# Layer 0's mixture of experts computed by lists of chosen tokens instead of for every token and expert

## The chip, the cores and the metric

The kernel runs on one core of a Trainium2 chip. A core has five engines that run side by side, each with its own queue of instructions: PE (TensorE, matmuls), DVE (VectorE), ACT (ScalarE), POOL (GpSimd) and SP (SyncE, which here mostly issues DMA). The metric is the device time of one execution in microseconds (us), the median over several runs. Times inside an execution come from a hardware profile of one further execution, counted from the start of its span.

## The reference

The whole is a decoder of four layers over 1024 tokens (8 blocks of 128, in two halves of 512) of 128 features. Each layer is an attention, a cross attention and a feed-forward part, and after each comes a sum with the input and a layer norm. The part that changes is layer 0's feed-forward part, a mixture of 8 experts of which each token uses two:

```python
def _L0_ffn_ref(x, router_w, w13, w2):
    E, H, I, K = (8, 128, 256, 2)
    logits = jnp.einsum('bsh,eh->bse', x, router_w)
    probs = jax.nn.softmax(logits, axis=-1)
    weights, indices = jax.lax.top_k(probs, K)
    weights = weights / (weights.sum(axis=-1, keepdims=True) + 1e-06)
    h13 = jnp.einsum('bsh,ehi->bsei', x, w13)
    gate, up = jnp.split(h13, 2, axis=-1)
    h = jax.nn.silu(gate) * up
    y = jnp.einsum('bsei,eih->bseh', h, w2)
    y_sel = jnp.take_along_axis(y, indices[..., None], axis=2)
    return (y_sel * weights[..., None]).sum(axis=2)
```

Layer 2 has a mixture of the same kind (8 experts, two per token, inner width 448). After layer 0's mixture come layer 1's attention over rotated vectors (`a1` in the code) and its cross attention with 16 heads (`x1`, computed by `attention16`).

## The kernel before, in words

Only PE's order is written out by hand (`manual_schedule(engines={PE})` around `first_layers`): PE runs in the order of the program. The queues of the other engines are put in order by the compiler, which takes the order of the program as priority and its own estimate of when an operand is ready. An instruction that waits holds up everything behind it on its engine.

**Layer 0's cross attention**, `ContextAttention`, runs in 35 units, u = 0 to 34, four for each block of 128 tokens; its last three only fold the last block's heads together and norm half 1 (L391 and L345 to L351 on DVE).

**Layer 0's mixture**, `FirstExperts` (L864 to L912), is dense: all 8 experts for all tokens, as 16 items, an expert and a half of 512 tokens each. `up` makes four matmuls with 512 columns (L889 to L891), a silu on ACT (L893) and a product on DVE (L894). `down` makes 8 matmuls of 128 columns (L904), and DVE adds the four results times the router's weight, zero where the expert isn't chosen, to an accumulator (L907). The weights come in four DMAs of 768 KB long before they are used. `top2` makes the router's weights. Items 0 to 3 run in the units u = 31 to 34; then a loop over k = 4 to 16 does one item's `up` and the item before's `down` in each step, and has other work between: x0's second turn after k = 5, the second half's routing, layer 1's 4-bit weights (`wq`) and constants after k = 6, the norm of half 0 after k = 8, and layer 1's rotated attention for half 0 (`a1.project`, `values`, `scores`, `turned`, `outputs`, `f.turn`) after k = 9 to 15. After the loop come `moe.norm(1)` and `x1.queries(0)`, then `attention16`, whose callback `between` holds half 1 of `a1`.

**Layer 2's mixture**, `ListedExperts` (L915 to L1126), takes only chosen pairs of a token and an expert, for each half on its own:

- `rows` writes the half's 512 input rows to DRAM. `route` finds each token's two experts. `places` counts by matmuls how many tokens chose each expert, and gives each pair a slot in a list in which every expert's part begins at a multiple of 128: at most N8 = 15 items of 128 rows. Its one-hot tiles `s16` and `r16` go into `lists`, whose 8 matmuls turn them into the ids of the rows of each item, and which then issues 15 gathers on POOL (L1030), an indirect DMA of 128 rows each into `e_xg` (8 buffers).
- For an item, `loaded` reads the expert's number into a register of SP and loads that expert's weights (L1043, four items ahead), `turned` transposes the gathered rows (L1060) and copies them by ACT (L1065), `up` and `down` compute the expert (silu L1075, product L1077), and the result goes to DRAM (L1088).
- `sums` gathers each token's two results back, 8 gathers on POOL (L1114), and 8 operations on DVE add them by weight to the input (L1122).

`run` (L1090) does the 30 items with other steps between them, among them `sums(0)` after item 17.

Of the kernel before, what the change touches and what calls it, by code (L numbers as in the profile page):

```python
# [21 lines left out]
B = 8  # L22
# [120 lines left out]
C2 = M2 // 4  # L143
W2COLS = 2 * M2 + 4 * D
# [10 lines left out]
W0COLS = 2 * I0 + 2 * D  # L155
# [3 lines left out]
def tile_decoder(  # L159
# [293 lines left out]

    def top2(xt, rw, eps, bs=range(B)):

        n = len(bs)

        def few(tag, shape, bufs=2):
            return small.tile(shape, F32, tag=f"{tag}{n}", name=tag, bufs=bufs)

        lg = ps_out.tile([P, n, 8], F32, tag="out", name="ps_lg")
        for k, b in enumerate(bs):
            mm(lg[:, k, :], tok(xt, b), rw)
        pr = softmax8(lg)
        shape = [P, n, 8, 8]
        other = pr.unsqueeze(2).to_broadcast(shape)
        own = pr.unsqueeze(3).to_broadcast(shape)
        gt = work.tile([P, B, 8, 8], F32, tag="g_gt", name="g_gt", bufs=1)[:, :n]
        nc.vector.tensor_tensor(gt, other, own, ALU.is_gt)
        eq = work.tile([P, B, 8, 8], F32, tag="g_eq", name="g_eq", bufs=1)[:, :n]  # L470
        nc.vector.tensor_tensor(eq, other, own, ALU.is_equal)
        eqf = eq.rearrange("p b e j -> p b (e j)")
        nc.vector.tensor_tensor(eqf, eqf, repeat(cst("tri"), n), ALU.mult)
        nc.vector.tensor_tensor(gt, gt, eq, ALU.add)
        rank = few("g_rank", [P, n, 8])
        nc.vector.tensor_reduce(rank, gt, AX.X, ALU.add)
        sel = few("g_sel", [P, n, 8])
        nc.vector.scalar_tensor_tensor(sel, rank, 2.0, pr, ALU.is_lt, ALU.mult)
        sm = few("g_sm", [P, n])
        nc.vector.tensor_reduce(sm, sel, AX.X, ALU.add)  # L480
        if eps:
            nc.vector.tensor_scalar_add(sm, sm, eps)
        rs = few("g_rs", [P, n])
        nc.vector.reciprocal(rs, sm)
        w = few("g_w", [P, n, 8], 8 // n)
        nc.vector.tensor_tensor(w, sel, spread(rs, 8), ALU.mult)
        return w
# [376 lines left out]
    class FirstExperts:  # L864


        def __init__(self, pool, x, xT):
            self.pool, self.xT, self.hT = pool, xT, {}
            self.f = Finish(x, of=third)
            self.acc = tile_of(pool, "e_acc", [P, B, D], bufs=1)  # L870
            nc.gpsimd.memset(self.acc, 0.0)
            self.w, self.loaded = {}, {}

        def load(self):
            for e in range(0, E0, 2):
                t = stream.tile([P, 2, W0COLS], F32, tag="w", name="w_moe0")
                nc.sync.dma_start(out=t, in_=w_moe0[:, e : e + 2, :])
                self.loaded[e // 2] = t

        def route(self, i):  # L880
            self.w[i] = top2(self.xT, msc("rw0"), 1e-6, range(4 * i, 4 * i + 4))

        def up(self, k):
            i, e = divmod(k, E0)
            t = self.loaded[e // 2][:, e % 2, :]
            h = tile_of(self.pool, "e_h", [P, 2, 512])
            for c in range(2):
                pg = ps_mm.tile([P, 512], F32, tag="mm", name="ps_g")
                mm(pg, t[:, c * P : (c + 1) * P], half(self.xT, i))  # L889
                pu = ps_sc.tile([P, 512], F32, tag="sc", name="ps_u")  # L890
                mm(pu, t[:, I0 + c * P : I0 + (c + 1) * P], half(self.xT, i))  # L891
                g = tile_of(self.pool, "e_g", [P, 512])
                nc.scalar.activation(g, pg, AF.Silu)  # L893
                nc.vector.tensor_tensor(h[:, c, :], g, pu, ALU.mult)  # L894
            self.hT[k] = h

        def down(self, k):
            i, e = divmod(k, E0)
            h = self.hT.pop(k)
            down = self.loaded[e // 2][:, e % 2, 2 * I0 :].rearrange("p (c d) -> p c d", d=D)  # L900
            po = ps_out.tile([P, 4, D], F32, tag="out", name="ps_o")
            for j in range(4):
                for c in range(2):
                    mm(po[:, j, :], h[:, c, j * T : (j + 1) * T], down[:, c, :], c == 0, c == 1)  # L904
            for j in range(4):
                a = self.acc[:, 4 * i + j, :]
                nc.vector.scalar_tensor_tensor(  # L907
                    a, po[:, j, :], self.w[i][:, j, e : e + 1], a, ALU.mult, ALU.add
                )

        def norm(self, i):
            self.f.norm(i, self.acc[:, 4 * i : 4 * i + 4, :])  # L912


    class ListedExperts:  # L915

# [42 lines left out]
        def places(self, i):  # L968
# [36 lines left out]
            for j in range(1, 4):  # L1005
                for k in range(2):
                    nc.gpsimd.tensor_scalar(self.r16[:, 4 * k + j, 1, :], item[:, 4 * k + j, :], float(j), None, ALU.mult)
            for k in range(2):
                nc.gpsimd.memset(self.r16[:, 4 * k, 1, :], 0.0)
# [1372 lines left out]
```

## Time and profile before

| | us |
|---|---|
| median of 11 runs | 875.99 (871.75 to 881.05) |
| the profiled execution's own time | 876.89 |
| its span | 875.1 |
| mean TensorE clock granted | 0.923 of full speed |
| busy over the span: PE | 724.7 (83%) |
| DVE | 545.2 (62%) |
| ACT | 418.5 (48%) |
| POOL | 177.6 (20%) |
| x0's last norm, from the folding's end to the normed rows | 165.8 to 173.4 |
| attention16's first scores | 251.49 |
| layer 2's last down ends | 690.0 |
| layer 2's mixture, normed rows of half 1 | 708.32 |

A line of the trace's timeline gives start and duration in us, the engine, the line of the source (helpers have one line for all their uses: L297 is every matmul, L329 a transpose of four), the output and the inputs by their names in the program, shapes, and how many such instructions are taken together. In square brackets stands how long the engine stood idle before it, and what ended that. PE is matmuls, PEld its loads of weights. A clock of 0.98 is the mean that the throttle granted in a stretch, as a share of full speed.

### The profile page before, as it was taken

The page shows a single profiled execution, that of the slowest core. Times are in us where ns is not written, and L with a number is a line of the kernel's source. Part 1 is how long each engine was busy: PE and PEld are TensorE (multiplying, and loading weights), DVE is VectorE, ACT ScalarE, POOL GpSimd, SP SyncE. Part 2 cuts the span into 40 slices and gives each one's busy share as a digit, 9 for nine tenths or more (in the row PEclk, how much of TensorE's full clock was granted, in tenths as well). Part 3 has the DMA queues.
Part 4 walks back from the last instruction along what each step waited for, and adds up shares of the span by engine and source line. Part 5 has one row for each costly group of instructions (what it writes and reads, how often), then busy time and mean ns, then how long its engine had stood idle before and what let it go on. Part 6 is the DMA issues. An engine that isn't in the chain of part 4 may idle for free. (4 is left out here: it accounts for less than half of the span.)

```text
span 875.1 us, 14577 instructions
## 1 busy us (share of the span) xinstructions
PE 724.7 (83%) x4790; PEld 497.1 (57%) x4790; DVE 545.2 (62%) x1561; ACT 418.5 (48%) x963; POOL 177.6 (20%) x373
## 2 busy tenths in 40 slices
PE   8789999999988687349888879769998869888883
PEld 4678776665655444125345445458997626655552
DVE  4767786674476665888777766653324166656663
ACT  3233455333566663454186555625334323566662
POOL 1400000010011300001120203044442220066660
PEclk9779999999999799769999999979998979999998
DMA  9310000000000000000000000056897274011111
GB/s 356 124 37 1 1 1 1 1 1 0 1 1 1 1 1 1 1 0 1 0 1 1 1 1 1 13 190 174 265 300 219 76 304 188 1 34 35 36 34 41
DMA packets 22771, 53.57 MB, mean 61 GB/s; under 512 B 3904, under 2 KB 14144, under 8 KB 21280
## 3 DMA queue, kind: packets, MB, share of 16 engines
q1 hardware_dynamic: 20640, 47.55, 16.2%
q0 software_dynamic: 1472, 3.02, 1.4%
q10 hardware_dynamic: 576, 2.00, 0.6%
q8 instruction: 39, 0.64, 0.3%
q14 instruction: 44, 0.36, 0.1%
HBM read 46.39 MB, written 3.01 MB: 56 GB/s over the span
## 5 line engine op out<-in xcount | busy, mean ns | idle before, releaser
L534 DVE TENSOR_REDUCE at_mx<-ps_s 128x8 f32<-128x1024 f32 x48 | 56.9, 1218 | 42.2 <-PE ps_s L297 42.2
L537 ACT ACTIVATE at_s<-ps_s,at_mx 128x128 f32<-128x128 f32 x192 | 53.7, 389 | 38.1 <-DVE at_mx L534 38.1
L297 PE MATMUL ps_o<-w_moe,e_h 128*128 128x128 f32 (+1 forms) x496 | 64.6, 279 | 8.6 <-DVE e_h L1077 5.9
L297 PEld LDWEIGHTS ps_o<-w_moe,e_h 128*128 128x128 f32 (+1 forms) x496 | 61.0, 194 | 17.0 <-issue 8.6
L546 ACT ACTIVATE at_pT<-ps_T 128x512 f32<-128x512 f32 x96 | 53.8, 601 | 34.3 <-PE ps_T L329 34.0
L329 PE MATMUL ps_T<-const_sb,at_s 128*128 128x128 f32 x384 | 61.9, 300 | 6.9 <-ACT at_s L537 5.1
L297 PE MATMUL ps_idle<-begin_bf 128*128 128x512 bf16 x226 | 63.9, 423 | 3.2 <-DVE l_s L658 2.2
L2119 POOL COPY l_wg<-w 128x64 f32 x192 | 48.6, 299 | 82.9 <-ACT l_wd L2115 54.5
L329 PEld LDWEIGHTS ps_T<-const_sb,at_s 128*128 128x128 f32 x384 | 47.5, 149 | 28.6 <-issue 10.7
L297 PEld LDWEIGHTS <-begin_bf 128*128 128x128 bf16 x273 | 28.0, 111 | 62.3 <-issue 41.9
L1077 DVE TENSOR_TENSOR e_h<-e_g,ps_u 112x512 f32<-112x512 f32 x30 | 20.6, 688 | 57.8 <-PE ps_u L297 45.4
L297 PEld LDWEIGHTS ps_acc<-l_wd,l_h 128*128 128x128 f32 x256 | 31.0, 191 | 38.5 <-ACT l_h L2141 38.5
L297 PE MATMUL ps_acc<-l_wd,l_h 128*128 128x128 f32 x256 | 37.1, 288 | 13.3 <-ACT l_h L2141 13.3
L805 ACT ACTIVATE x_p<-ps_s,x_mx 128x256 f32<-128x256 f32 x64 | 30.0, 475 | 33.7 <-DVE x_mx L801 26.1
L517 POOL TENSOR_TENSOR kx<-xa_k,const_sb 128x512 f32<-128x512 f32 x16 | 16.8, 1054 | 130.1 <-PE ps_s L297 74.0
L2115 ACT COPY l_wd<-w 64x128 f32 x96 | 28.5, 297 | 26.1 <-PE ps_acc L297 19.1
L297 PE MATMUL ps_s<-kvT,x_q 128*128 128x256 f32 x128 | 35.6, 404 | 4.0 <-ACT x_p L805 4.0
L297 PE MATMUL ps_av<-at_pT,vaug 128*32 128x128 f32 x768 | 31.1, 284 | 9.0 <-ACT at_pT L546 8.5
L335 ACT ACTIVATE sd<-ln_mv,eps 128x4 f32<-128x4 f32 x28 | 8.3, 298 | 62.7 <-DVE ln_mv L346 55.3
L894 DVE TENSOR_TENSOR e_h<-e_g,ps_u 128x512 f32<-128x512 f32 x32 | 21.8, 685 | 24.0 <-PE ps_u L297 20.8
L893 ACT ACTIVATE e_g<-ps_g 128x512 f32<-128x512 f32 x32 | 19.0, 597 | 34.2 <-PE ps_g L297 28.1
L1030 POOL DMA_INDIRECT e_xg<-l_rows,e_ids x30 | 29.1, 971 | 29.3 <-PE ps_T L1060 16.3
(481 smaller groups left out, 1720.4 us busy)
## 6 DMA issues: line engine op xcount, KB each, us to landing
w_moe<-in_w_moe_dram SPq DMA_DIRECT2D x30, 704.0 KB
w<-in_w_moe_dram SPq DMA_DIRECT2D x10, 1024.0 KB
w_moe<-in_w_moe_dram SPq DMA_DIRECT2D x4, 768.0 KB
l_wd<-w SPq DMA_DIRECT2D x96, 32.0 KB
l_out<-e_y SPq DMA_DIRECT2D x30, 64.0 KB
sq_sb<-in_squares_dram SPq DMA_DIRECT2D x1, 1152.0 KB
row_sb<-in_rows_dram ACTq DMA_DIRECT2D x1, 784.0 KB
const_sb<-in_consts_dram ACTq DMA_DIRECT2D x1, 630.5 KB
```

What stands on the lines that cost most here:

```text
L297: nc.tensor.matmul(dst, lhsT, rhs, start=start, stop=stop)
L329: nc.tensor.transpose(ps[:, i, :], src[:, i, :], ident)
L534: nc.vector.tensor_reduce(nmx[k], flat, AX.X, ALU.max, negate=True)
L537: nc.scalar.activation(sh[u][1][:, i // 4, i % 4, :], flat[:, i, :], AF.Identity, bias=nmx[1][:, i : i + 1])
L546: to_T(sh[u][g // 2][:, g % 2], lambda t: nc.scalar.activation(p, t, AF.Exp))
L805: nc.scalar.activation(pr[:, j, :], ps[:, j, :], AF.Exp, bias=mx[:, j : j + 1], accum_out=sm[:, j : j + 1])
L893: nc.scalar.activation(g, pg, AF.Silu)
L894: nc.vector.tensor_tensor(h[:, c, :], g, pu, ALU.mult)
L1030: nc.gpsimd.indirect_dma_start(out=xg, out_offset=None, in_=self.rows_d[i], in_offset=bass.IndirectOffsetOnAxis(ap=self.ids[i][:, o : o + ...
L1077: nc.vector.tensor_tensor(self.h[k], g, pu[:C2], ALU.mult)
L2115: nc.scalar.copy(dst, src)
L2119: nc.gpsimd.tensor_copy(dst, src)
```

## The change

`FirstExperts` and `top2` go. `ListedExperts` gets the inner width and the size of a chunk as arguments and serves both layers. For layer 0 an item is 128 gathered rows: a load of 384 KB, a transpose, 4 up matmuls and 2 down matmuls of 128 columns; 30 items for the two halves. The gathered rows of the second half get buffers of their own, 12 of them, in both layers (before, both halves shared 8). The `r16` products move from POOL to DVE, `s16` comes after them. `run` becomes `step(k)`, and `first_layers` places the steps:

```diff
-                    if u == 21:
-                        moe = FirstExperts(pool_of("l0f", 2, "right"), x0.f.x, x0.f.xT)
-                        moe.load()
-                    if u == 22:
-                        moe.route(0)
...
+                    if u == 18:
+                        moe.rows(0, xin[:, 0:4, :])
+                    elif u == 22:
+                        moe.route(0, x0.f.xT)
+                    elif u == 25:
+                        moe.places(0)
+                    elif u == 28:
+                        moe.lists(0)
                     if u >= 4 * B - 1:
-                        moe.up(u - 4 * B + 1)
-                        if u >= 4 * B:
-                            moe.down(u - 4 * B)
+                        moe.step(u - 4 * B + 1)
+                moe.rows(1, xin[:, 4:8, :])
+                moe.weights_of(0)
                 x1 = None
-                for k in range(4, 2 * E0 + 1):
-                    if k < 2 * E0:
-                        moe.up(k)
-                    moe.down(k - 1)
+                for k in range(4, 2 * N8 + 1):
+                    moe.step(k)
                     if k == 5:
                         x0.f.turn(1)
                     elif k == 6:
-                        moe.route(1)
+                        moe.route(1, x0.f.xT)
...
-                    elif k == 8:
-                        moe.norm(0)
-                    elif k == 9:
-                        moe.f.turn(0)
                     elif k == 10:
-                        a1.project(0)
-                        a1.values(0)
-                    elif k == 11:
-                        a1.scores(0)
+                        moe.places(1)
...
+                        x1.keys(0)
                     elif k == 12:
-                        a1.turned(0)
-                        x1.keys(0)
-                    elif k == 13:
-                        a1.outputs(0)
-                    elif k == 15:
-                        a1.f.turn(0)
-                        x1.biased(0)
-                moe.norm(1)
+                        moe.second = pool_of("l0g", 1, "right")
+                        moe.lists(1)
+                        x1.keys(1)
+                    elif k == N8 + 2:
+                        f.norm(0, moe.sums(0, xin[:, 0:4, :]))
+                        moe.weights_of(1)
+                    elif k == N8 + 11:
+                        f.turn(0)
+                    elif k == N8 + 12:
+                        a1.project(0)
+                        a1.values(0)
+                    elif k == N8 + 13:
+                        a1.scores(0)
+                f.norm(1, moe.sums(1, xin[:, 4:8, :]))
+                idle(6)
+                a1.turned(0)
+                a1.outputs(0)
+                idle(20)
+                a1.f.turn(0)
+                x1.biased(0)
                 x1.queries(0)
...
-                        (0, 1): (lambda: x1.keys(1),),
-                        (0, 2): (lambda: moe.f.turn(1), lambda: a1.project(1)),
-                        (1, 0): (lambda: a1.values(1),),
+                        (1, 0): (lambda: f.turn(1), lambda: a1.project(1), lambda: a1.values(1)),
```

`idle(n)` puts n matmuls on PE whose result nobody reads. Inside `ListedExperts`, for both layers:

```diff
-            self.s16 = work.tile([P, 8, P], BF16, tag="g_gt", name="e_s16", bufs=1)
-            nc.vector.tensor_tensor(self.s16, spread(s, P), repeat(tidx, 8), ALU.is_equal)
...
-            nc.gpsimd.tensor_scalar(self.r16[:, :, 0, :], item, cst("index"), None, ALU.mult)
-            for j in range(1, 4):
-                for k in range(2):
-                    nc.gpsimd.tensor_scalar(self.r16[:, 4 * k + j, 1, :], item[:, 4 * k + j, :], float(j), None, ALU.mult)
...
+            nc.vector.tensor_scalar(self.r16[:, :, 0, :], item, cst("index"), None, ALU.mult)
+            nc.vector.tensor_tensor(
+                self.r16[:, :, 1, :].rearrange("p (k j) o -> p k j o", j=4),
...
+            nc.vector.tensor_tensor(self.s16, spread(s, P), repeat(tidx, 8), ALU.is_equal)
...
-                self.xg[N8 * i + o] = xg = self.few("xg", [P, D], bufs=8)
+                self.xg[N8 * i + o] = xg = (self.second if i else self.pool).tile(
+                    [P, D], F32, tag=f"e_xg{i}", name="e_xg", bufs=12 if i else 8
+                )
...
-            t = stream.tile([P, 1, W2COLS], F32, tag="w", name="w_moe8")
+            t = stream.tile([P, 1, 2 * self.inter + self.n * D], F32, tag="w", name="w_moe8")
```

In the new code the loads of an item's weights are issued four items ahead, as in layer 2, from the four big loads' place at the kernel's start nothing is left. The host packs layer 0's weights by expert as it did layer 2's.

## The prediction

> **What bounds the kernel now.** I first read the windows view over the two mixtures: layer 0's dense one (from the end of the units without mixture, 146.50, to attention16's first scores, 251.49) and layer 2's, which already runs by lists.
>
> ```profile
> core 0: us, PE busy (x) PEld busy (x) DVE busy (x) ACT busy (x) POOL busy (x), PEclk, DMA share, GB/s
> 146.50:251.50 105.00, 101.64 (x477) 64.76 (x476) 63.02 (x189) 47.04 (x78) 5.51 (x11) 0.98 0.00 1
> 592.00:690.00 98.00, 88.69 (x773) 86.71 (x772) 33.30 (x86) 40.10 (x96) 34.94 (x41) 0.96 0.74 226
> ```
>
> The dense stage is PE's alone: 101.64 of 105.00 us busy at clock 0.98, no DMA. Everything else hides behind it. The listed stage uses DMA at 0.74 and POOL for a third. I therefore price the new stage with layer 2's rows. The PE timeline gives one dense item (176.12 back to the same point of the previous one, 170.91: 5.21 us), the second block one listed item of layer 2 (2.75 us).
>
> ```profile
> 174.34 1.95 PE L297 MATMUL ps_o<-w_moe,e_h 128*128 128x128 f32 x16
> 176.12 1.02 PE L297 MATMUL ps_g<-x_T,w_moe 128*128 128x512 f32 x2
> 176.99 1.02 PE L297 MATMUL ps_u<-x_T,w_moe 128*128 128x512 f32 x2
> ```
>
> ```profile
> 669.52 0.28 PE L1060 MATMUL ps_T<-const_sb,e_xg 128*128 128x128 f32 x1
> 669.63 1.03 PE L297 MATMUL ps_g<-e_xT,w_moe 128*112 128x128 f32 x8
> 670.51 1.04 PE L297 MATMUL ps_u<-e_xT,w_moe 128*112 128x128 f32 x8
> 671.38 1.06 PE L297 MATMUL ps_o<-w_moe,e_h 112*128 112x128 f32 x8
> 672.27 0.27 PE L1060 MATMUL ps_T<-const_sb,e_xg 128*128 128x128 f32 x1
> ```
>
> A matmul counts as two entries (x8 for four), so the listed item is a transpose (0.11) and 12 matmuls of 0.22.
>
> **What PE loses.** 16 dense items × 5.21 = 83.4 us go. 30 listed items with 256 inner columns come: 0.11 + (4 up + 2 down) × 0.22 = 1.43, × 30 = 42.9. PE sheds 40.5 us. Would the rest keep up, the kernel would end near 836. So I follow the chain of results that no longer hides.
>
> **A. Units 18 to 30 (to 146.5).** Places and lists of half 0 are new there: PE +0.36 and +0.42 (their matmuls in layer 2), DVE +4.0 net (4.9 for places' row in layer 2 with s16 on top, less the 0.9 of the weights that go and the adds that move). DVE is busy 20.28 of the 24.1 us from 122, so some 4 us are free, but not always where they are wanted. Bounds 0.8 (PE alone) to 6 (all of DVE in the way); I take 2: first item at 148.5.
>
> **B. To the end of x0's folding.** x0's own PE part is 5.4; steps 0 to 2 are 3.96 (three items, their first down later). End 148.5 + 9.4 = 157.9, against 165.8 now.
>
> **C. To the second half's ids.** The chain is a row of links that layer 2 and layer 0 show: norm of half 1, 165.8 to 173.4 now, 7.6 (PE has only steps 3 to 5, 4.3, so it stands 3.4 us ahead of the turn); turn 1.2; step 6, 1.43; route 0.8; then PE's wq transposes 2.5, steps 7 to 10 5.7 and the exp/silu table pair 2 (the item around such a pair in layer 2 took 4.67 instead of 2.75), 10.2 together, which is more than route's DVE chain of 7.0 (187.0 to 194.03 now); places 0.36; its chain to s16 4.9 (613.9 to 618.8); lists 0.42; ids 0.75. Sum 27.7: ids at 185.7 (t0).
>
> **D. To the last down.** POOL's queue now holds 15 row gathers of half 1 (12 free buffers, so the first 12 start at once) and then sums(0)'s 8. A gather costs POOL 0.95 and 0.30 between, 1.25; 23 × 1.25 = 28.75. The whole-engine timeline of layer 2 shows what hangs behind them:
>
> ```profile
> 652.17 0.35 DVE L1122 SCALAR_TENSOR_TENSOR fin_h<-e_y,e_w,l_xx 128x128 f32<-128x128 f32 x1 [2.24 <-DMA e_y<-l_out,e_place]
> ...
> 655.20 0.35 DVE L1122 SCALAR_TENSOR_TENSOR fin_h<-e_y,e_w,l_xx 128x128 f32<-128x128 f32 x1 [2.68 <-DMA e_y<-l_out,e_place]
> 656.42 0.94 POOL L1114 DMA_INDIRECT e_y<-l_out,e_place  x1 [0.30 <-issue]
> ...
> 659.90 0.69 DVE L1077 TENSOR_TENSOR e_h<-e_g,ps_u 112x512 f32<-112x512 f32 x1 [2.48 <-remote]
> ...
> 660.65 0.58 PE L297 MATMUL ps_o<-w_moe,e_h 112*128 112x128 f32 x1 [5.46 <-DVE e_h L1077]
> ```
>
> Adds that wait for gathers stand ahead of e_h in DVE's queue, and PE stood 5.46 us. In the new stage an item is half as long, so the gathers are later against PE. From the last gather's start to the norm's end layer 2 takes 6.1 (702.24 to 708.32): f.norm(0) ends at t0 + 27.5 + 6.1 = t0 + 34. PE has by then only steps 13 to 26 (20 us): it stands 13 us, in pieces of an add each. Then turn 1.2, steps 27 to 30 5.7, project 1.73, values 0.9, scores 0.9, the last item's lag 1.5: t0 + 46 = 231.7. PE's work alone would be 29 (all of it without a wait), the bound from below; 48.5 with more of it at the low clock.
>
> **E. The tail, to attention16.** Now sums(1) gathers after the last down, where before there was no gather at all. DVE in layer 2's tail (last down ended at 690.0):
>
> ```profile
> 696.01 0.35 DVE L1122 SCALAR_TENSOR_TENSOR fin_h<-e_y,e_w,l_xx 128x128 f32<-128x128 f32 x1 [7.27 <-DMA e_y<-l_out,e_place]
> ...
> 702.25 0.35 DVE L1122 SCALAR_TENSOR_TENSOR fin_h<-e_y,e_w,fin_h 128x128 f32<-128x128 f32 x1 [0.39 <-DMA e_y<-l_out,e_place]
> 702.52 0.18 DVE L346 BATCH_NORM_AGGREGATE ln_mv<-ln_st 128x2 f32<-128x6 f32 x1
> 702.61 0.65 DVE L1850 TENSOR_TENSOR l_u<-l_g,ps_proj 64x512 f32<-64x512 f32 x1
> ...
> 704.71 0.35 DVE L1122 SCALAR_TENSOR_TENSOR fin_h<-e_y,e_w,fin_h 128x128 f32<-128x128 f32 x1 [0.74 <-DMA e_y<-l_out,e_place]
> ```
>
> Eight adds, each waiting for its gather, until 14.7 us after the last down; layer 3's product, whose operands were there by 696, ran behind six of them. So I put a1's norm behind the adds too: 14.7 + its 5.0 (242.14 to 247.17 now) + 4.3 from there to attention16 (247.17 to 251.49) = 24. If DVE has a1's operations first, it is 235.91 to 247.17, 11.3, + 4.3 = 16 (the other bound). I take 24, because program order has the sums first and the row shows such an order. attention16 then begins at 255.7, 4.2 later.
>
> **F. Behind it.** attention16's first unit now waits 2.69 (258.55) with norm(1)'s operations among its maxima; keys(1) leaves it as well: −1.5 (0 to −2.7). Layer 2: the ring of 12 takes an e_xg gather (655.17) out of sums(0)'s middle, −1.5 (−5, the wait whole, to 0); the r16 products on DVE ≤ 0.7 in the same place, beside DVE that is busy a third of the stage. Weights: 30 × 384 KB and as many 64 KB writes and gathers; layer 2 moved 317 GB/s at most, 1.6 us an item, just above PE's 1.43, hidden by the waits of C and D. More code is fetched beside busy DMA; layer 2 has holes "issue" of 0.4 to 1.3 there: +1 (0 to 7).
>
> **Sum.** +4.2 − 1.5 − 1.5 + 1 = +2.2. The profiled execution took 876.89 (span 875.1 and 1.8 around it), 0.9 over the median 875.99. 875.99 + 2.2 = **878**. About 0.3%, 2.6 us, is what a measurement of this kernel can tell from no change.
>
> **The clock, row first.** After one wait of 1.54 us the next pairs ran at half speed for 3.5 us:
>
> ```profile
> 206.98 1.22 PE L329 MATMUL ps_T<-const_sb,x_nat 128*128 128x128 f32 x4 [1.54 <-DVE x_nat L351]
> 208.00 1.92 PE L297 MATMUL ps_g<-x_T,w_moe 128*128 128x512 f32 x2
> 209.70 1.79 PE L297 MATMUL ps_u<-x_T,w_moe 128*128 128x512 f32 x2
> ```
>
> 1.92 and 1.79 instead of 1.02: about 2 us lost. [...]
>
> **Rivals.**
> 1. *The tail isn't blocked*: E is 16. For it: a1's chain is on the path and its operands come from 6 us on, while adds come one per 1.25. Against: 702.61 above. −8: **870**. Chance 0.24.
> 2. *No wait in D*: sums(0)'s gathers get ahead of the last row gathers, or DVE lets e_h pass. For it: the 655.17 gather stood among e_y's, so that order isn't strict. PE's work 29 plus half of the 17 that waits: −9 to −11: **868**, with rival 1 860. Chance 0.12.
> 3. *Slower: the clock falls through D and stays low.* PE stands an add at a time from step 20; if each wait costs as at 206.98, steps 27 to 30, project, values and scores (9.4 us) run at half speed, and attention16's start too (2). Price 9.4 + 2 = 11 on top: **889**. It decides as soon as waits of 1.5 us come more often than every 5 us; against it stands 660.65, one long wait and then recovery. Chance 0.20.
> 4. *The change doesn't do what it says in layer 2*: the ring moves no gather and layer 2 stays as it is: 878 + 1.5. It moves the sum little, and has no chance of its own.
>
> **Chances.** The forecast 0.36 (own range 873 to 886, for A, E's links and code), rival 1 0.24, rival 2 0.12, rival 3 0.20, 0.08 for anything else, half on each side. Faster by over 0.3%: nine tenths of rivals 1 and 2 (0.32), a tenth of the forecast (0.04), 0.04: 0.40. Within: four tenths of the forecast and the rest of rivals 1 and 2: 0.18. Slower: half of the forecast (0.18), rival 3 (0.20), 0.04: 0.42. The range goes from 861 (both rivals 1 and 2 at their weaker end) to 892 (rival 3 with code at +4).
>
> **What will show it.** A: first e_xT transpose at 148.5. C: second half's first gather near 186. D: PE standing for DVE's e_h or for x_nat between the 17th and 27th item, 13 us in all, with fin_h adds waiting on e_y. E: fin_h of sums(1) ahead of a1's norm on DVE, attention16's first scores at 255 to 256. Layer 2: 592 to 690 shorter by 1 to 2. The forecast is wrong if PE has no wait over 3 us in D, if the tail is 16, or if the granted clock in the stage is below 0.9.

## The result and the profile after

The changed kernel takes 914.05 us (median of 12 runs, 909.65 to 917.4), the kernel before 876.06 in the runs beside it (46). The ratio is 1.0437, 95% interval 1.042 to 1.0454: slower by 38 us, where 878 with a range of 861 to 892 was forecast. The profiled execution took 915.89 (span 914.0); its clock was 0.900 (0.923 before), POOL was busy 217.0 us (177.6 before), PE 707.6 (724.7 before).

PE is busy 17.1 us less; 40.5 were forecast, at full clock, and part of the new work ran at half clock (the granted clock was 0.64 from 200 to 220, below). At full clock the timeline of PE shows a listed item of layer 0, transpose to transpose, in 233.10 − 231.65 = 1.45 us (forecast 1.43):

```profile
231.65 0.27 PE L975 MATMUL ps_T<-const_sb,e_xg 128*128 128x128 f32 x1
...
233.10 0.27 PE L975 MATMUL ps_T<-const_sb,e_xg 128*128 128x128 f32 x1
```

What isn't as forecast is seen in the windows view of the stage (columns: window and length, then busy time and count of each engine, the granted clock, DMA share and rate):

```profile
160.00:200.00 40.00, 30.34 (x252) 27.06 (x253) 25.92 (x90) 22.80 (x58) 15.69 (x22) 1.00 0.68 185
200.00:220.00 20.00, 2.39 (x16) 1.66 (x15) 0.55 (x2) 0.82 (x3) 15.12 (x17) 0.64 0.46 76
220.00:240.00 20.00, 15.27 (x105) 14.47 (x106) 8.09 (x30) 9.69 (x30) 0.73 (x1) 0.76 0.65 186
240.00:280.00 40.00, 25.43 (x140) 15.72 (x139) 14.37 (x53) 12.62 (x40) 8.82 (x9) 0.80 0.16 48
```

From 200 to 220 PE, DVE and ACT together do almost nothing, and only POOL works. The timeline of all engines shows the hole itself:

```profile
199.25 0.61 PE L294 MATMUL ps_g<-e_xT,w_moe 128*128 128x128 f32 x4
...
199.69 0.61 PE L294 MATMUL ps_u<-e_xT,w_moe 128*128 128x128 f32 x4
...
204.84 0.71 PE L294 MATMUL ps_g<-e_xT,w_moe 128*128 128x128 f32 x4 [1.96 <-issue]
...
205.39 0.71 PE L294 MATMUL ps_u<-e_xT,w_moe 128*128 128x128 f32 x4
206.03 0.94 POOL L945 DMA_INDIRECT e_xg<-l_rows,e_ids  x1 [0.30 <-issue]
...
212.11 0.38 ACT L990 ACTIVATE e_g<-ps_g 128x256 f32<-128x256 f32 x1 [7.32 <-remote]
...
219.78 0.95 POOL L1026 DMA_INDIRECT e_y<-l_out,e_place  x1 [0.30 <-issue]
219.88 0.42 DVE L992 TENSOR_TENSOR e_h<-e_g,ps_u 128x256 f32<-128x256 f32 x1 [17.87 <-remote]
...
220.35 1.23 PE L294 MATMUL ps_o<-w_moe,e_h 128*128 128x128 f32 x4 [14.25 <-issue]
...
225.03 0.40 ACT L990 ACTIVATE e_g<-ps_g 128x256 f32<-128x256 f32 x1
...
225.46 0.42 DVE L992 TENSOR_TENSOR e_h<-e_g,ps_u 128x256 f32<-128x256 f32 x1 [5.16 <-ACT e_g L990]
```

Counted off item by item, ACT's operation at 212.11 takes the `ps_g` that ended at 199.86, and DVE's at 219.88 the `ps_u` that ended at 200.30. The groups at 204.84 and 205.39 belong to the next item, which ACT and DVE take up at 225.03 and 225.46. The trace's semaphore events agree with this count: there are twelve signals of PE for the twelve results that ended between 198.4 and 221.8, and those of the first two groups come at 212.09 and 219.78. So ACT and DVE were ready and were told late, by 12.2 and 19.5 us. Meanwhile POOL issues one gather after the other, 1.25 us apart, the last at 219.78. Six signals then come together, from 224.69 to 224.93, and from 226.43 on they are prompt again. I call this "late results" below. The view's own words mislead here: "issue" at PE and "remote" at DVE are what is left when no releaser is found.

Where the 38.9 us of span come from, by points that both traces have; the last column is the same for a pair of runs without late results (after_3 against dense_plain, see below):

| stretch | before | after | difference | without late results |
|---|---|---|---|---|
| start to attention16's first scores | 251.5 | 276.5 | +25.0 | +9.8 |
| to layer 1's first sigmoid | 107.1 | 112.3 | +5.2 | +4.1 |
| to layer 2's first gather | 225.1 | 226.8 | +1.7 | +0.7 |
| layer 2's mixture to its last norm | 123.5 | 132.8 | +9.3 | +3.4 |
| the rest | 167.9 | 165.5 | −2.4 | +1.1 |

### The profile page after: what moved, and what is told of

It reads as the page before. It is cut to its first block, busy times and chain, and to the rows that moved or that the text cites. A ratio compares the mean times of both kernels' runs of the same rounds, so it can differ in the third digit from the quotient of the medians.

```text
span 914.0 us, 15117 instructions
## 1 busy us (share of the span) xinstructions
PE 707.6 (77%) x4866; PEld 500.5 (55%) x4866; DVE 533.6 (58%) x1559; ACT 420.0 (46%) x1020; POOL 217.0 (24%) x400
## 5 line engine op out<-in xcount | busy, mean ns | idle before, releaser
L992 DVE TENSOR_TENSOR e_h<-e_g,ps_u 128x256 f32<-128x256 f32 (+1 forms) x60 | 33.1, 551 | 122.2 <-PE ps_u L294 61.3
L945 POOL DMA_INDIRECT e_xg<-l_rows,e_ids x60 | 58.7, 978 | 116.6 <-DVE e_ids L940 72.4
L294 PE MATMUL ps_o<-w_moe,e_h 112*128 112x128 f32 (+1 forms) x360 | 54.6, 291 | 23.2 <-issue 17.2
L294 PE MATMUL ps_g<-e_xT,w_moe 128*112 128x128 f32 (+1 forms) x360 | 55.0, 292 | 12.9 <-ACT e_xT L980 5.4
L294 PEld LDWEIGHTS ps_o<-w_moe,e_h 112*128 112x128 f32 (+1 forms) x360 | 48.3, 204 | 25.4 <-issue 18.2
L326 PEld LDWEIGHTS ps_T<-const_sb,at_s 128*128 128x128 f32 x384 | 46.1, 146 | 28.3 <-issue 10.4
L294 PE MATMUL ps_u<-e_xT,w_moe 128*112 128x128 f32 (+1 forms) x360 | 54.7, 290 | 4.0 <-issue 3.6
L294 PEld LDWEIGHTS ps_g<-e_xT,w_moe 128*112 128x112 f32 (+1 forms) x360 | 48.8, 198 | 14.7 <-ACT e_xT L980 5.7
L294 PEld LDWEIGHTS ps_u<-e_xT,w_moe 128*112 128x112 f32 (+1 forms) x360 | 48.5, 196 | 5.9 <-issue 5.9
L1026 POOL DMA_INDIRECT e_y<-l_out,e_place x32 | 30.3, 947 | 76.6 <-DMA l_out<-e_y 63.8
L990 ACT ACTIVATE e_g<-ps_g 128x256 f32<-128x256 f32 (+1 forms) x60 | 29.6, 494 | 35.9 <-PE ps_g L294 16.0
```

The lines of the kernel that those rows point to most:

```text
L294: nc.tensor.matmul(dst, lhsT, rhs, start=start, stop=stop)
L326: nc.tensor.transpose(ps[:, i, :], src[:, i, :], ident)
L945: nc.gpsimd.indirect_dma_start(out=xg, out_offset=None, in_=self.rows_d[i], in_offset=bass.IndirectOffsetOnAxis(ap=self.ids[i][:, o : o + ...
L990: nc.scalar.activation(g, pg[:ch], AF.Silu)
L992: nc.vector.tensor_tensor(self.h[k], g, pu[:ch], ALU.mult)
L1026: nc.gpsimd.indirect_dma_start(out=y, out_offset=None, in_=self.out_d[i], in_offset=bass.IndirectOffsetOnAxis(ap=self.place[i][:, 4 * k + ...
```

## The experiments

All ratios are to the kernel before on the same chip, with 95% intervals.

**Is it the gathers, the code, or the data?** Three explanations stood against each other: POOL's back-to-back gathers disturb how PE's results reach others; new code is fetched late; the rows arrive late. Four kernels, one chip. Two add to the kernel before one write of rows to DRAM and then 23 transfers into tiles that nobody reads, in the middle of its dense stage, as indirect gathers by POOL or as plain loads by SP:

```diff
                     if k == 5:
                         x0.f.turn(1)
...
+                        for o in range(23):
+                            t = spare.tile([P, D], F32, tag="spare_t", name="spare_t", bufs=8)
+                            nc.gpsimd.indirect_dma_start(
+                                out=t, out_offset=None, in_=spare_d,
+                                in_offset=bass.IndirectOffsetOnAxis(ap=at[:, 0:1], axis=0),
+                            )
```

dense_plain has `nc.sync.dma_start(out=t, in_=spare_d[T * (o % 4) : T * (o % 4 + 1), :])` there.

> The kernel before (dense mixture in layer 0) with 23 row gathers on POOL added, back to back, whose rows nobody reads, in the middle of the dense stage that PE fills. Theory 1 (while POOL gathers back to back, other engines learn late that a matmul is done; in the changed kernel 23 such gathers held the stage up by 14 to 17 us): 8 to 18 us longer than before, though nothing waits for the gathers. Theory 2 (the stop is made by work that waits for the gathers' data, or by the order of the queues): within 1 us of before. Theory 3 (code or data loads are late beside busy DMA): the same as with 23 plain transfers of the same size.

> The kernel before with the same 23 transfers of 64 KB added in the same place, unread, but as plain DMAs issued by SP from the same tensor. Theory 1 (gathers alone do it): within 1 us of before. Theory 3 (DMA traffic beside it): as much longer as with the gathers.

listed_plain_rows is the changed kernel whose second half in layer 0 takes its rows by plain loads, so other rows than the lists name; l0_ring_4 gives those rows 4 buffers instead of 12, so that a gather is issued only when an item frees a buffer:

```diff
-                    [P, D], F32, tag=f"e_xg{i}", name="e_xg", bufs=12 if i else 8
+                    [P, D], F32, tag=f"e_xg{i}", name="e_xg", bufs=(self.ring if i else 8)
```

> The changed kernel, but layer 0's second half takes plain stretches of 128 rows by SP in place of its 15 gathered rows (so these items compute other rows than the lists say; all else is as it was). Theory 1: the stop of 14 us at 205 goes, only 8 gathers are left before the tail: 12 to 18 us less than the changed kernel, 896 to 902. Theory 2 (the stop comes from sums(0) and its order): less than 4 us gained. Theory 3: the same bytes move, so nothing gained, within 2 us.

> The changed kernel with 4 instead of 12 buffers for the second half's rows in layer 0, so that after the fourth a gather waits for an item's transpose, and sums(0)'s gathers come between them. Theory 1: gathers at one per item's pace don't hold up the rest: 6 to 15 us less than the changed kernel. Theory 2: sums(0) comes later and PE waits for it at the turn: 0 to 6 us more.

Measured: dense_gathers 0.9994 (0.9971 to 1.0017), dense_plain 0.9995 (0.9986 to 1.0005), listed_plain_rows 1.0147 (1.0111 to 1.0183), l0_ring_4 1.0152 (1.013 to 1.0175). The unread gathers cost nothing, which spoke against the first explanation; and yet both changed kernels without the burst of 12 ended 13 us over before instead of 38, which spoke for it. One thing hadn't been foreseen: the kernel before took 869.36 on this chip, not 876.06. So the chip itself might differ.

**The pieces, on a chip like the first.** On the next chip the kernel before took 876.61. after_again is the changed kernel as it is. l2_ring_8 gives layer 2 back its shared 8 buffers (`self.few("xg", [P, D], bufs=8)`). turn_earlier splits the callback in attention16 as it was before:

```diff
-                        (1, 0): (lambda: f.turn(1), lambda: a1.project(1), lambda: a1.values(1)),
+                        (0, 2): (lambda: f.turn(1), lambda: a1.project(1)),
+                        (1, 0): (lambda: a1.values(1),),
```

before_ring_4 is the kernel before with 4 instead of 8 buffers for layer 2's rows, and nothing else.

> The changed kernel once more, beside the kernel before on this chip. In the run with plain rows and the one with 4 buffers no matmul was told of late, in layer 2 neither, whose 12 gathers in a row were as in the changed kernel. Theory 1 (a long row of gathers beside the loads of the weights makes PE's results known late): the stop of 14 us at 205 is there again, 4.4% over the kernel before. Theory 4 (it was a state of the chip on which the changed kernel was first timed): no such stop, within 0.5% of the 1.5% that the run with 4 buffers took over the kernel before.

> The changed kernel with layer 2's rows in the shared ring of 8 again, layer 0 as changed. Theory 1: layer 2's stage gets back the 9 us that it lost (12 gathers in a row, then PE's results late): 7 to 10 us less than the changed kernel in the same call. Theory 4: without late results the ring matters little in layer 2: within 3 us of the changed kernel in the same call.

> The changed kernel with the turn and the projection of a1's half 1 back in attention16's first unit, where they stood before; the values stay in the second. If the 5 us that attention16 lost come from the turn, the projection and the values in one place (PE waits 3.3 for the turn's copy): 3 to 5 us less than the changed kernel in the same call. If they come from the clock after the tail's wait: within 1 us of it.

> The kernel before with 4 instead of 8 buffers for layer 2's gathered rows, so that fewer gathers run back to back. Theory 1: PE's late results at 594, 626 and 651 go: 2 to 6 us less than before, if the chip shows them at all. Theory 4 (on a chip without late results): gathers come later, 0 to 3 us more.

Measured: after_again 1.0416 (1.0366 to 1.0467); l2_ring_8 1.0328 (1.0267 to 1.0388), with layer 2 at 125.4 instead of after_again's 133.0; turn_earlier 1.0371 (1.0309 to 1.0434), with attention16 to layer 1's sigmoid at 107.4, before's length; before_ring_4 **0.9931** (0.991 to 0.9951), with layer 2 at 119.5 instead of 123.5. So pacing alone makes the kernel before faster on this chip. In the profiled executions (875.1 and 867.9 us, before's from the first timing) 4.0 us of it lie in layer 2 and 2.3 behind its last norm, where neither trace has a late signal; those 2.3 aren't explained. POOL's timeline shows the pacing, of before and then of before_ring_4:

```profile
622.87 0.95 POOL L1030 DMA_INDIRECT e_xg<-l_rows,e_ids  x1 [0.30 <-PE ps_u L297]
624.12 0.95 POOL L1030 DMA_INDIRECT e_xg<-l_rows,e_ids  x1 [0.30 <-PE ps_T L1060]
625.38 0.94 POOL L1030 DMA_INDIRECT e_xg<-l_rows,e_ids  x1 [0.31 <-issue]
626.62 0.95 POOL L1030 DMA_INDIRECT e_xg<-l_rows,e_ids  x1 [0.30 <-issue]
```

```profile
621.03 0.95 POOL L1030 DMA_INDIRECT e_xg<-l_rows,e_ids  x1 [1.74 <-PE ps_T L1060]
623.78 0.95 POOL L1030 DMA_INDIRECT e_xg<-l_rows,e_ids  x1 [1.81 <-PE ps_T L1060]
```

A gather every 1.25 us in the first, every 2.75 us in the second. For the results that ended between 624 and 628.3 before's PE signals came 0.8 to 3.3 us late; from 630 to 648, with gathers 2.75 us apart, they were prompt. before_ring_4 still has late results, up to 9.2 us, for what ended between 646 and 657: there `sums(0)`'s gathers, which the ring doesn't pace, are 1.25 us apart.

turn_earlier also shows what the callback cost. PE's timeline of after and of turn_earlier at the turn:

```profile
290.53 0.66 PE L326 MATMUL ps_T<-const_sb,x_nat 128*128 128x128 f32 x4 [0.25 <-ACT at_pT L508]
294.44 3.68 PE L294 MATMUL ps_proj<-x_T,l_rot 128*128 128x512 f32 x4 [3.25 <-ACT x_T L406]
```

```profile
291.29 0.66 PE L326 MATMUL ps_T<-const_sb,x_nat 128*128 128x128 f32 x4
292.63 1.98 PE L294 MATMUL ps_proj<-x_T,l_rot 128*128 128x512 f32 x4 [0.68 <-ACT x_T L406]
```

The projection needs the turn's copy, which on ACT stands behind other work; PE waited 3.25 us for it and then ran the projection at half speed, 3.68 instead of 1.98.

**Do chips differ?** The same gathers and the same ring on a third and fourth chip, with versions that also mend the tail. tail_later has 4 buffers in both layers, the callback of turn_earlier, and `sums` split, so that half 1's adds stand behind a1's own norm in the program:

```diff
-                f.norm(1, moe.sums(1, xin[:, 4:8, :]))
+                moe.fetch(1)
                 idle(6)
                 a1.turned(0)
                 a1.outputs(0)
+                f.norm(1, moe.added(1, xin[:, 4:8, :]))
```

a1_inside is tail_later with `f.turn(0)`, the projection, scores, turn and outputs of a1 two steps earlier among the items, and norm(1) and the turn inside attention16.

> The kernel before with 23 unread gathers in the dense stage, as before in dense_gathers, which ran on a chip whose traces show no late results of PE at all. If this chip shows late results (the kernel before near 876): theory 1a (gathers in a row make PE's results late whatever else runs): results late by 1 us and more between 175 and 208, the stage 1 to 18 us longer. Theory 1b (it takes the weights' loads and the rows' writes beside the gathers): no late results there, within 2 us of before. If it doesn't (before near 869): the same as in dense_gathers, within 1 us.

> The changed kernel with 4 buffers for layer 0's second half, once more. On a chip with late results (before near 876): theory 1 (a long row of gathers): the stop of 14 us goes, 15 to 25 us less than the changed kernel's 913.6, 889 to 899, with layer 2's 9 us still lost. If the number of buffers has nothing to do with it: 910 or more. On a chip without them: 1.5% over before, as the first time.

> The changed kernel with 4 buffers for the second half's rows in layer 0, the shared ring with 4 in layer 2, a1's turn and projection of half 1 back in attention16's first unit, and the adds of sums(1) put behind a1's outputs in the program (its gathers stay where they are). If the tail of 24 us comes from the adds ahead of a1's norm on DVE: the time from the last down to attention16's scores becomes 16. If from something else: it stays at 24. In all, beside l0_ring_4_2 in the same call: 8 for the tail, 4 for the turn, and 6 more for layer 2 where the chip shows late results: 12 to 18 us less.

> As tail_later, but a1's chain of half 0 (turn, projection, values, scores, turned, outputs) stands among the second half's items from step 24 on, as soon as norm(0) is there, in place of behind them, and norm(1) and the rest of half 1 stand in attention16. If the critical path is gathers of sums(0), norm(0), a1's chain (t0 + 34 + 20): attention16's first scores 52 to 56 us after the second half's first gather, before 70 to 82, and less in all than the kernel before by 2 to 12 us. If sums(1)'s gathers and adds hold attention16's first maxima up (DVE has them ahead): 4 to 10 us of that are lost in attention16's first unit.

Before took 870.29 here. Measured: dense_gathers_2 0.998 (0.996 to 1.0), l0_ring_4_2 1.0179 (1.0143 to 1.0216), tail_later 1.0034 (1.0009 to 1.006), a1_inside 1.0138 (1.0098 to 1.0178). The gathers cost nothing again. tail_later brings the tail from 24.1 to 16.07 us, the bound that the prediction had for an unblocked DVE. a1_inside lost: attention16 to the sigmoid took 118.9 instead of 110.0, and it didn't begin earlier either (first scores at 253.80 against 251.99).

> The changed kernel once more. It was timed so far on chips on which the kernel before takes 876 and PE's results come late beside rows of gathers. On a chip on which the kernel before takes 869 to 870: theory 4 (the late results are the chip's, and cost the changed kernel more than the one before): no stop at 205, D (second half's first gather to the last down) 44 to 50 instead of 60, layer 2 from its first gather to its last norm 119 to 121 instead of 133, in all 1.3% to 2% over the kernel before. Theory 1 (any chip, by the 12 buffers): 4% over it, with the stop.

> As tail_later, but sums(0)'s gathered results of layer 0 share a ring of 6 with the second half's rows, so that they come one for each item from step 24 on, and a1's turn, projection and scores of half 0 stand behind the last item. If the adds that wait ahead of e_h are what holds D up (10 us of stops and 4 at half clock in the run with 4 buffers): no stop of PE over 1.5 us between the second half's first gather and the last down, that stretch 28 to 34 instead of 46, scores at 54 to 60 after the first gather instead of 63: 3 to 9 us less than tail_later's 0.34% over the kernel before, so 0.2 to 0.7% under it; on a chip with late results 0.9 to 1.5% under it. If norm(0) comes later by as much as D gets shorter: as tail_later, within 2 us.

one_ring is tail_later with the results of half 0 gathered into the rows' ring of 6, so that the 8 result gathers are paced too, and turn, projection and scores behind the last item:

```diff
+                    if self.own and i == 0:
+                        y = self.second.tile([P, D], F32, tag="e_xg1", name="e_y", bufs=6)
+                    else:
+                        y = self.late(f"y{k}", [P, D], bufs=4)
...
-                        f.norm(0, moe.sums(0, xin[:, 0:4, :]))
                         moe.weights_of(1)
...
+                    elif k == N8 + 9:
+                        f.norm(0, moe.sums(0, xin[:, 0:4, :]))
```

On this fourth chip before took 868.75 and the unchanged after **889.29**: 1.0222 (1.0175 to 1.027), half the loss of the first timing. one_ring 1.0069 (1.0042 to 1.0095), where a gain was expected: from the second half's first gather to the last down it took 41.9 us instead of 28 to 34, with stops of 2.11 and 1.89 for the items' weights and of 2.17 for `e_h`. In after_3 the hole of 14 us is gone, though POOL issues the same burst:

```profile
200.00:220.00 20.00, 8.75 (x56) 8.16 (x55) 3.74 (x14) 4.12 (x11) 12.45 (x14) 0.74 0.80 177
```

What is left is the wait that the prediction had in D. The whole-engine timeline of after_3:

```profile
206.63 0.94 POOL L1026 DMA_INDIRECT e_y<-l_out,e_place  x1 [0.30 <-issue]
...
213.73 0.61 DVE L1034 SCALAR_TENSOR_TENSOR fin_h<-e_y,e_w,x_nat 128x128 f32<-128x128 f32 x2 [12.78 <-DMA e_y<-l_out,e_place]
...
214.26 0.41 DVE L992 TENSOR_TENSOR e_h<-e_g,ps_u 128x256 f32<-128x256 f32 x1
...
214.73 1.22 PE L294 MATMUL ps_o<-w_moe,e_h 128*128 128x128 f32 x4 [10.21 <-DVE e_h L992]
```

DVE's queue has the add first, it waits for a gather that POOL issues behind the second half's row gathers, and `e_h` behind it keeps PE 10.21 us.

**The deciding run**: the unread gathers, which cost nothing on two chips, on a chip where before takes 875.83, together with l0_ring_4.

> The kernel before with 23 unread gathers in its dense stage. On a chip with late results: theory 1a (gathers in a row are enough) has results late by 1 us and more between 175 and 208 and 1 to 18 us more in the stage; theory 1b (the weights' loads beside them are needed) none, within 2 us of before. On a chip without: as before, within 1 us.

> The changed kernel with 4 buffers for layer 0's second half. On a chip with late results (the kernel before near 876): theory 1 (a long row of gathers) has 889 to 899 instead of the changed kernel's 913.6, and no stop of 14 us at 205; if the buffers have nothing to do with it, 910 or more. On a chip without (869 to 870): 1.5 to 1.8% over the kernel before, as twice already, against 2.2% of the changed kernel.

Measured: dense_gathers_3 **1.0207** (1.0106 to 1.0307), l0_ring_4_3 1.033 (1.027 to 1.039). The same kernel text, whose gathers nobody reads, loses 18 us here (its three runs 888.5, 898.7 and 902.27) and nothing there. PE's timeline of dense_gathers, without late results, at the `wq` transposes:

```profile
186.69 0.85 PE L637 MATMUL ps_T<-const_sb,wq_q 128*128 128x128 f32 x6
188.11 0.55 PE L637 MATMUL ps_T<-const_sb,wq_q 128*128 128x128 f32 x3 [0.57 <-ACT quantT L294]
```

The same place in dense_gathers_3, all engines:

```profile
185.27 0.85 PE L637 MATMUL ps_T<-const_sb,wq_q 128*128 128x128 f32 x6
...
194.36 0.48 ACT L294 COPY quantT<-ps_T 128x384 f32<-128x384 f32 x1 [11.74 <-remote]
...
194.89 0.90 PE L637 MATMUL ps_T<-const_sb,wq_q 128*128 128x128 f32 x3 [8.77 <-issue]
```

0.57 us between the transposes in one, 8.77 in the other. The copy by ACT waits for transposes that ended at 186.1 by the timeline; PE's signals of these us come at 185.79, 189.38, 191.51, 194.33 (that of these transposes), 199.96 and 204.19, then four from 207.01 to 207.25; from 208.29 on they are prompt. POOL's last gather began at 202.37. (This profiled execution is the one of 888.5.) No data of the gathers is used, and the dense weights had been there for long. So it isn't the data. l0_ring_4_3, 1.5% to 1.8% on the other chips, loses 3.3% here, more than the 889 to 899 us expected: its layer 2, with the ring of 12, takes 129.6 against 119.4 in l0_ring_4, and attention16's first scores come at 267.9 against 258.6, so the ring of 4 doesn't keep layer 0 free of late results (up to 6.0 us in its trace).

> The kernel before with 4 buffers instead of 8 for layer 2's gathered rows, once more. On a chip with late results (before near 876): again 0.5 to 0.9% less. On a chip without them (869 to 870): if the gain was only fewer late results, within 0.2% of before; if it was something else about the order, 0.5% less here too.

> The best variant of the listed mixture so far (4 buffers in both layers, a1's turn of half 1 earlier, the adds of sums(1) behind a1's outputs), which took 0.3% more than the kernel before on a chip without late results. There again 0.1 to 0.6% more. On a chip with late results: layer 0's own gathers still cost some 10 (as in the run with 4 buffers, 3.3% over), layer 2's 6 come back: 1 to 2% over the kernel before.

On a further chip, before 875.85: before_ring_4_2 0.9934 (0.9912 to 0.9957), so the gain of before_ring_4 holds; tail_later_2 1.0054 (1.0033 to 1.0075), less than the 1% to 2% expected. The ratio is near the 1.0034 of the third chip, the time isn't: 881.94 against 873.30, and 11.9 over before_ring_4_2 beside it. The ratio is small because before itself has late results here. tail_later_2's trace has them too, up to 8.4 us between 200 and 227, where its gathers are still mostly 1.25 us apart, and up to 9.5 in layer 2. So pacing takes away part of what such a chip costs, not all.

## Why the prediction was wrong, point by point

**The sum: two causes, one foreseen in kind.** The chips fall into two kinds: before takes 868.75 to 870.29 on three, whose traces show no late results, and 875.83 to 876.61 on three others and in the first timing (on one of these or a fourth), whose traces all show them. After minus before is 20.5 us on the first kind (889.29 − 868.75) and 38 on the second. So about 18 of the 38 us are late results, a term that the prediction didn't have; the other 20, of which 2.2 were forecast, are steps that were mis-sized. That it's the gathers that bring the late results out is shown by dense_gathers_3 (added, with one plain write ahead of them: +2.07%) and before_ring_4 (spread out: −0.7%, twice). Plain transfers in their place were tried only on a chip of the first kind (dense_plain). The trace of after answers a part of that; in these 8 us (columns as above) it has plain transfers at a DMA share of 0.90 and nothing on POOL, and PE's signals come 0.01 to 0.02 us after the ends:

```profile
233.00:241.00 8.00, 7.02 (x61) 6.63 (x60) 4.93 (x21) 6.13 (x17) 0.00 (x0) 1.00 0.90 262
```

What makes one chip do it and another not, no run here shows; each chip was used once, so the chip and its state at that time can't be told apart. Nor is it settled whether the matmul itself ends late or only the news of it. The signals at 212.09 and 219.78 against ends at 199.86 and 200.30 show that the timeline's end alone can't be read as the result's time; which of the two was late they don't show.

**Its step "F … More code is fetched beside busy DMA; … +1 (0 to 7)"** is the one that failed by mechanism. I took layer 2's holes marked "issue" for code on its way and gave them +1; late results took about 18. In after no instruction was fetched between 193.0 and 229.4, the whole hole included. The holes in the trace of before were late results already (signals 0.4 to 9.2 us behind the matmuls' ends, at 593 to 600, 624 to 629 and 650 to 664), and I passed over them: layer 2 of the kernel before is 4 us shorter with paced gathers.

**The row that step D rests on** was misread in the same way. The `e_h` at 659.90 takes a `ps_u` that ended at 651.88, and the last adds ahead of it were done at 657.42; before's timeline of all engines has

```profile
650.85 1.04 PE L297 MATMUL ps_u<-e_xT,w_moe 128*112 128x128 f32 x8
...
656.81 0.61 DVE L1122 SCALAR_TENSOR_TENSOR fin_h<-e_y,e_w,l_xx 128x128 f32<-128x128 f32 x2 [1.26 <-issue]
```

and PE's signal for that `ps_u` only came at 659.81. So the last 2.48 of PE's 5.46 us were a late result, and the adds set at most the rest. That adds do hold up `e_h` is shown by after_3, not by this row; there was some luck in it.

**A and B.** First transpose at 151.3 (148.5 forecast, bounds 147.3 to 152.5): that DVE's new work was more in the way than I took is the likely reason, but no run isolates it. B 10.4 in after_3 (9.4 forecast), 14.1 in after, whose trace has late results there too.

**C.** 26.8 us in both, 27.7 forecast. The links of layers 2 and 0 added up.

**D.** 46 forecast (29 to 48.5): 50.0 in after_3, 46.0 in l0_ring_4 on a chip of the same kind, 60.2 in after with late results. The mechanism, adds ahead of `e_h`, is the wait of 10.21 above; it stood in one piece, not an add at a time. One detail failed: `f.turn(0)` waited for nothing. (Of t0 + 34, with 20 us of steps, PE would stand 14 us, not 13; the 46 doesn't depend on it.)

**E.** 24.1 measured (252.4 to 276.5), 24 forecast. The alternating order on DVE is as assumed. After's timeline of DVE:

```profile
259.55 0.35 DVE L1034 SCALAR_TENSOR_TENSOR fin_h<-e_y,e_w,x_nat 128x128 f32<-128x128 f32 x1 [0.76 <-DMA e_y<-l_out,e_place]
...
262.21 0.34 DVE L393 SCALAR_TENSOR_TENSOR fin_h<-ps_o,l_rd,x_nat 128x128 f32<-128x128 f32 x1
...
268.24 0.35 DVE L1034 SCALAR_TENSOR_TENSOR fin_h<-e_y,e_w,fin_h 128x128 f32<-128x128 f32 x1 [0.57 <-DMA e_y<-l_out,e_place]
...
272.33 1.11 DVE L348 TENSOR_SCALAR x_nat<-fin_h,ln_mv,rstd 128x128 f32<-128x128 f32 x4
```

a1's L393 comes one by one between adds that wait, and its norm ends behind the last. tail_later has the four together, and its norm before the adds are done:

```profile
244.37 1.13 DVE L393 SCALAR_TENSOR_TENSOR fin_h<-ps_o,l_rd,x_nat 128x128 f32<-128x128 f32 x4
...
247.56 1.36 DVE L348 TENSOR_SCALAR x_nat<-fin_h,ln_mv,rstd 128x128 f32<-128x128 f32 x4
...
251.87 0.35 DVE L1044 SCALAR_TENSOR_TENSOR fin_h<-e_y,e_w,fin_h 128x128 f32<-128x128 f32 x1 [0.30 <-DMA e_y<-l_out,e_place]
```

16.07 and 15.76 in its two runs: rival 1's price of 8 us was right, and it needed another order in the program.

**F.** attention16: −1.5 forecast, +5.2 measured; the callback that joins turn and projection makes up 3.4 of it (turn_earlier 107.4 beside after_again's 110.8 on the same chip). The step saw a wait that goes and not the new one between turn and projection. Layer 2: −1.5 forecast, +9.3 with late results, 0.1 to 3.4 without (119.3 in listed_plain_rows, 119.4 and 119.8 in l0_ring_4 and l0_ring_4_2, 122.6 in after_3, against dense_plain's 119.2; what after_3 has more than the others isn't known). The ring of 12, for which I had forecast a gain, is what lets POOL issue back to back; l2_ring_8 gives 7.6 of it back.

**Rival 3, the clock.** The windows from 200 to 280 have 0.64 to 0.80 in after, so the low clock is there, but it follows the holes and isn't what makes them: by the trace's records of the granted clock it was half from 205.77 to 229.66, and the first `ps_g` that came late by 12.2 us had ended at 199.86 at full clock. Rival 3's price was an estimate from the one row at 206.98. Two other runs have such stops. PE's timeline of l0_ring_4:

```profile
216.50 1.22 PE L294 MATMUL ps_o<-w_moe,e_h 128*128 128x128 f32 x4 [2.53 <-DVE e_h L993]
...
220.48 0.71 PE L294 MATMUL ps_o<-w_moe,e_h 128*128 128x128 f32 x4 [0.90 <-DVE e_h L993]
```

and of one_ring:

```profile
215.68 1.22 PE L294 MATMUL ps_o<-w_moe,e_h 128*128 128x128 f32 x4 [1.12 <-DVE e_h L993]
...
222.99 0.71 PE L294 MATMUL ps_o<-w_moe,e_h 128*128 128x128 f32 x4 [2.17 <-DVE e_h L993]
```

By the traces' records of the granted clock the half clock ran from 215.98 to 219.40 in l0_ring_4, around the end of a stop of 2.53, and from 215.25 to 218.66 in one_ring, around the end of one of 1.12 that came after two of 2.11 and 1.89; a stop of 2.17 brought none. So the length of a stop alone doesn't tell whether the half clock comes. In the records of before and after each stretch of half clock lasts 3.41 us or a multiple of it (the last, which the end cuts short, left out); by what it is set off no run here shows.

**Rival 2** (no wait in D) and **rival 4** didn't come about; rival 4's "layer 2 stays as it is" is near the truth on chips without late results.

**The 20 us without late results.** To attention16 the loss was +9.8 (the forecast's +4.2, A and B +3.2, C −0.9, D +3.9, and −0.6 because before itself is later on that chip), then attention16 +4.1, layer 2 +3.4 and 1.8 beyond. PE was busy 24.8 us less (718.5 in dense_plain, 693.7 in after_3), and its waits took more than that: each of the 23 + 8 gathers costs POOL 1.25 us, and in D and in the tail PE waits for adds that wait for gathers, as the rows above show. The best version with lists, tail_later, is 0.3% to 0.5% slower than before, and 1.4% slower than before_ring_4_2 on the chip where both ran; of all versions run only before_ring_4 is faster, 0.7%, on chips with late results, the only ones where it was run.

## What to carry to other kernels

In the stage that moved from PE to lists of gathered rows, the chain of the gather queue (count times its pitch, 23 × 1.25 us) and the queue position of the adds behind it (10.21 us of PE's waiting in after_3) set the time, not PE's work; reckon with both before such a move. Issue gathers one per item by a small ring, not in a burst by a large one: in layer 2, with items of 2.75 us, this paid (119.5 us instead of 123.5 in before_ring_4); in layer 0, with items of 1.45, a ring of 4 still left late results on such a chip (up to 6.0 us in l0_ring_4_3). And put adds that wait for gathers behind work that is ready (the tail in tail_later took 16.07 us, 24.1 in after). Where a trace has holes "issue" on PE and "remote" on others, look at when PE's signals come before blaming code or data, and time a kernel on more than one chip.

## What was not expected of the hardware

PE's results reached ACT and DVE up to 21.9 us after the matmuls' ends (in after a down result that ended at 202.78 was taken up at 224.71), while POOL issued indirect gathers 1.25 us apart, on chips where the kernel before takes 876 us; the traces of the three chips where it takes 869 to 870 show none of it. In after's hole signals to PE weren't late: PE started within 0.06 us of the end of DVE's late `e_h` (219.88, 0.42 long; PE at 220.35) and of ACT's `e_xT` (224.87, 0.27 long; PE at 225.19). Between 602 and 643 in before_ring_4, with gathers 2.75 to 3.7 us apart, no signal was late, and 23 unread gathers cost 0, 0 and 18 us on three chips.
